# Sparse neighbour aggregation on one core: the adjacency matrix cut into units of 256 rows by all columns instead of 512 rows by half the columns

## The chip, the cores and the metric

The kernel runs on one core of one Trainium2 chip. The metric is device time in microseconds (us) of one execution, of which lower is better. A profiled execution gives a span (first to last instruction) that is a little shorter than that time.

## The reference

The inputs are node features `x` (4096 x 64), a dense adjacency matrix `adj` (4096 x 4096, fp32, only 0 and 1; 64 MB), a 64 x 64 weight and a bias. What is computed:

```python
h = relu(layernorm(x))
support = h @ weight                       # 4096 x 64
mask = (adj != 0)
rank = cumsum(mask, axis=1)
deg = rank[:, -1:]
k = minimum(deg, 100)
pos = rank - (deg - k)
w = mask * where(pos > 0, 0.5 ** (k - pos), 0.0)
out = x + (w @ support + bias)
```

So each neighbour is weighted by one half to the power of the number of neighbours to its right in the same row, and only the last 100 of a row count. The cumulative count along a row of 4096 columns is what couples the columns with each other.

## The kernel before

Nearly all of the data is `adj`. Row `r*2048 + p*16 + t` lies on partition p, so that one **tile** is 128 rows with the same `r` and `t` (32 tiles in all), and a partition's part of a tile is contiguous in memory.

The matrix is processed in 16 **units** of 512 rows (four tiles) by 2048 columns. For a group of 512 rows the right half of the columns comes first (the head), then the left half, since counts run from the right. For each unit:

- `load` (L120, SyncE queue): one 1 MB transfer for each tile, 8 KB on each partition, into one of 8 buffers (`a_sb`, pool `apool`). A load waits until the `convert` that read its buffer is done.
- `convert` (L341 on VectorE, L339 on ScalarE for three tiles): fp32 to one byte for each column, four columns to a word (`m8`, shown as `m`).
- `transpose` (L352, TensorE) turns 128 x 128 words through PSUM (`pt`), and `settle` (L363, VectorE) copies them to SBUF (`mt`): columns now lie on partitions, rows along the free axis.
- `totals` (L369) counts neighbours for each block of columns with matrix products; `split` (L379, ScalarE) and `divide` (L382, VectorE) each take one byte of the counts to fp16 (`sums`).
- `carry` (L388, GpSimd), in the left half alone, copies into a free row of `sums` what stands to the right of the unit, from the right half's `behind`.
- `suffix` (L396) adds up the later blocks with one matrix product for each byte, and `clamp` (L400, VectorE) makes the limited count `behind`.
- `place` (L407 and L412, TensorE), twice for a unit, forms the exponent codes in four PSUM banks (`v`, 5 buffers).
- `weigh` (L420, ScalarE), eight for a unit, takes two bytes of the code through Exp: 128 x 1024 weights (`wk`).
- `aggregate` (L453, TensorE), eight for a unit, multiplies the weights with `hr` (support as a high and a low fp32r part) into `acc`: two matrix products of 512 columns each.
- `drain`, `turn_back`, `finish` (L469, L476, L483 and L484) take each 512-row group out of PSUM, add x, and leave it for the stores.

Three of the last weighs (`QUICK`) are made on VectorE and GpSimd instead of ScalarE (`encode` L426, `take` L431, `lower` L439), and three others (`PARTED`) in halves of 256 rows. In front of all that stands a prologue (layer norm and support).

The order of the instructions on each engine is made in Python before the kernel is emitted: a planner holds for each step an engine, a duration and a due time, and always takes the step that can start soonest, among near ties the one due first. Each engine then works its list in order, so a step that waits holds up all behind it on its engine.

Of the kernel before, what the change touches and what calls it, by code (L numbers as in the profile page):

```python
# [29 lines left out]

@with_exitstack
def kernel(
# [12 lines left out]

# [7 lines left out]
    CB = HB // E  # L74
# [4 lines left out]
    G = RT // TG  # L79

    UNITS = [(g, c * P * E, n) for g in range(G) for c, n in ((4, 4), (0, 4))]
    U = len(UNITS)
    UT = [(u, tt) for u in range(U) for tt in range(TG)]
    NT = len(UT)
    POS = [sum(UNITS[v][2] for v, _ in UT[:n]) // 2 for n in range(NT + 1)]
    NP = 2 * CB
    QUICK = (U - 2, 4), (U - 1, 0), (U - 1, 4)
    PARTED = 5, 6, 7
    NA = 8
    NV = 5  # L90
    NB = 2
# [4 lines left out]
    bpool = ctx.enter_context(tc.tile_pool(name="bpool", bufs=6))  # L96
    mpool = ctx.enter_context(tc.tile_pool(name="mpool", bufs=3))
    wpool = ctx.enter_context(tc.tile_pool(name="wpool", bufs=NP + 4))
    dpool = ctx.enter_context(tc.tile_pool(name="dpool", bufs=2))
    bhpool = ctx.enter_context(tc.tile_pool(name="bhpool", bufs=3))  # L100
# [7 lines left out]


    tiles = {}  # L110
    xt = mpool.tile([P, CB, W, 2], F16, name="mt").rearrange("p c i e -> p (c i e)").bitcast(F32)
    xr = const.tile([P, H, HT, D], F32, name="xr")
    xr_v = x.rearrange("(r p t) d -> p r t d", r=H, t=HT)

    def load(n):
        u, tt = UT[n]
        g, c0, cb = UNITS[u]
        t = g * TG + tt
        tiles[n] = apool.tile([P, N // H], F32, tag="a_sb", name="a_sb")
        nc.sync.dma_start(tiles[n][:, :cb * E * P], adj_v[:, t // HT, t % HT, c0:c0 + cb * E * P])  # L120
# [9 lines left out]

# [13 lines left out]

    thr, later, excess = {}, {}, {}
    for cb in sorted({cb for g, c0, cb in UNITS}):
        thr[cb] = setup.tile([P, 4, SUB], F32, name=f"thr{cb}")
        later[cb] = const.tile([P, 2, P], F16, name=f"later{cb}")
        excess[cb] = const.tile([P, 1], F32, name=f"excess{cb}")
        nc.gpsimd.memset(thr[cb], 4096.0)  # L150
        nc.gpsimd.iota(thr[cb][:, :, 4:4 + 4 * cb].rearrange("p j (a f c) -> p j a f c", f=2, c=4),
                       pattern=[[1, 4]] + [[32, 2]] * (cb == CB) + [[16, 2], [4, 4]], base=0, channel_multiplier=0,
                       allow_small_or_imprecise_dtypes=True)
        nc.gpsimd.memset(thr[cb][:, :, 0:1], -1.0)
# [21 lines left out]

# [13 lines left out]
    over = setup.tile([P, 1], F16, name="over")  # L190
    nc.gpsimd.memset(over, 136.0)
    floor = const.tile([P, 1], F32, name="floor")
    nc.gpsimd.memset(floor, -38.0 * LN2)
# [4 lines left out]
    used = setup.tile([P, 2], F32, name="used")  # L198

    def order_of(cb):  # L200


        sub = setup.tile([P, 2], F32, name=f"sub{cb}")
        nc.vector.scalar_tensor_tensor(sub[:, 0:1], pf[:, 1:2], 8.0 if cb == CB else 2.0, pf[:, 3:4], op0=ALU.mult, op1=ALU.add)
        nc.vector.scalar_tensor_tensor(sub[:, 0:1], pf[:, 2:3], 0.125, sub[:, 0:1], op0=ALU.mult, op1=ALU.add)
        nc.vector.tensor_scalar(sub[:, 1:2], sub[:, 0:1], 16.0, None, op0=ALU.add)
        nc.vector.memset(sub[:1, 0:1], 4000.0)
        for f in range(2):
            nc.vector.tensor_scalar(later[cb][:, f, :], thr[cb].rearrange("p j r -> p (j r)"), sub[:, f:f + 1], used[:, f:f + 1],
                                    op0=ALU.is_lt, op1=ALU.mult)  # L210

    def constants(n):
        if n == 0:
            nc.vector.tensor_tensor(pi[:, 1:], pi[:, 0:1].to_broadcast([P, 5]), bits, op=ALU.bitwise_and)
            nc.vector.tensor_copy(pf, pi)
            nc.vector.tensor_scalar(used, pf[:, 5:6].to_broadcast([P, 2]), 8.0, None, op0=ALU.is_equal)
            nc.vector.memset(used[:1, 0:1], 1.0)

            nc.vector.tensor_scalar(one, row, 20.0, -1.0, op0=ALU.is_ge, op1=ALU.mult)
        elif n == 1:  # L220

# [15 lines left out]

# [8 lines left out]

# [3 lines left out]
    pxs, sqs, ns = {}, {}, {}  # L250

    def turn(h, t0):

# [9 lines left out]

        pxs[n] = ps_v.tile([P, W], F32, tag="v", name="pc")
        nc.tensor.matmul(pxs[n], less.rearrange("p h d -> p (h d)"), xt[:, n * W:(n + 1) * W], start=True, stop=True)  # L265

# [17 lines left out]

# [7 lines left out]

# [17 lines left out]
    def piece(h, i):  # L310
        return slice(h * HB + i * HB // 2, h * HB + (i + 1) * HB // 2)

    def first(h, i):
        nc.scalar.activation(hr[:, piece(h, i), 0, :], xs[:, piece(h, i), :], AF.Copy)

    def second(h, i):
        nc.vector.tensor_sub(hr[:, piece(h, i), 1, :], xs[:, piece(h, i), :], hr[:, piece(h, i), 0, :].bitcast(F32))

    def count(cb):
        r = SUB * cb  # L320
        px = pxs["count", cb] = ps_v.tile([P, W], F32, tag="v", name="pn")
        nc.tensor.matmul(px[:, :1], later[cb][:r, 1, :], over[:r], start=True, stop=True)
# [4 lines left out]

    low, codes, masks, words, wts, accs, tots, pts, sums8, behind, vs, signed = {}, {}, {}, {}, {}, {}, {}, {}, {}, {}, {}, (1, 7, 15)

    def convert(n):  # L330
        cb = UNITS[UT[n][0]][2]
        m8 = bpool.tile([P, CB * P, E], U8, name="m8")
        m_v, a_v = m8[:, :cb * P, :], tiles.pop(n)[:, :cb * P * E]
        if cb == CB:
# [3 lines left out]
        if n in signed:  # L338
# [3 lines left out]
        words[n] = m8  # L342

    def transpose(n, c0, c1):
        u, tt = UT[n]
        if tt == 0 and c0 == 0:
            masks[u] = mpool.tile([P, CB, W, 2], F16, name="mt")
        if c0 == 0:
            pts[n] = ps_t.tile([P, CB, P], F32, tag="t", name="pt")
        m32 = words[n].rearrange("p q e -> p (q e)").bitcast(F32)  # L350
        for c in range(c0, c1):
            nc.tensor.transpose(pts[n][:, c, :], m32[:, c * P:(c + 1) * P], ident)  # L352

    def settle(n):
        u, tt = UT[n]
        cb = UNITS[u][2]
        mw = masks[u].rearrange("p c i e -> p c (i e)").bitcast(U32)[:, :cb, tt * P:(tt + 1) * P]
        pt = pts.pop(n).bitcast(U32)[:, :cb, :]
        words.pop(n)
        if n in signed:  # L360
# [3 lines left out]

    def totals(u):
        tot = pts[u, "n"] = ps_t.tile([P, W], F32, tag="t", name="tot")
        for a in range(2):
            for c in range(UNITS[u][2]):
                nc.tensor.matmul(tot[SUB * c:SUB * (c + 1), :], band[:, SUB - 12 - 4 * a:2 * SUB - 12 - 4 * a],  # L369
                                 masks[u][:, c, :, a], start=(a == 0), stop=(a == 1), skip_group_check=True)  # L370

    def bytes_of(u, f):
        r = SUB * UNITS[u][2]
        if u not in sums8:
            sums8[u] = dpool.tile([P, 2, W], F16, name="sums8")
        return sums8[u][:r, f, :], pts[u, "n"][:r].bitcast(U8).rearrange("p (i f) -> p f i", f=4)[:, 1 + f, :]

    def split(u):
        nc.scalar.activation(*bytes_of(u, 0), AF.Copy)  # L379

    def divide(u):
        nc.vector.tensor_copy(*bytes_of(u, 1))  # L382

    def halved(u):
        pts.pop((u, "n"))

    def carry(u):
        nc.gpsimd.tensor_copy(sums8[u][:1, 0, :], behind[u - 1][:1, :])  # L388

    def suffix(u):  # L390
        cb = UNITS[u][2]
        r = SUB * cb
        sums = sums8.pop(u)
        px = pts[u, "s"] = ps_t.tile([P, W], F32, tag="t", name="ps")
        for f in range(2):
            nc.tensor.matmul(px, later[cb][:r, f, :], sums[:r, f, :], start=(f == 0), stop=(f == 1))  # L396

    def clamp(u):
        behind[u] = bhpool.tile([P, W], F16, name="behind")
# [295 lines left out]
```

## Time and profile before

The time is 190.65 us, median of 3 runs (190.29 to 190.69). The profiled execution has a span of 188.8 us.

| engine | busy us | share of the span | instructions |
|---|---|---|---|
| TensorE (PE) | 171.8 | 91% | 1499 |
| VectorE (DVE) | 161.7 | 86% | 221 |
| ScalarE (ACT) | 149.5 | 79% | 176 |
| GpSimd (POOL) | 20.4 | 11% | 60 |
| DMA | 69.49 MB moved | mean 368 GB/s | 10338 packets |

Busy time of TensorE counts the whole passage of each product, and products overlap, so TensorE is less full than its share says. A "mean ns" of a group is the time from start to end of one instruction; when the same engine goes on with the next, the distance from start to start is shorter. Both are given where they are used.

### The profile page before, as it was taken

The page shows a single profiled execution, that of the slowest core. Times are in us where ns is not written, and L with a number is a line of the kernel's source. Part 1 is how long each engine was busy: PE and PEld are TensorE (multiplying, and loading weights), DVE is VectorE, ACT ScalarE, POOL GpSimd, SP SyncE. Part 2 cuts the span into 40 slices and gives each one's busy share as a digit, 9 for nine tenths or more (in the row PEclk, how much of TensorE's full clock was granted, in tenths as well). Part 3 has the DMA queues.
Part 4 walks back from the last instruction along what each step waited for, and adds up shares of the span by engine and source line. Part 5 has one row for each costly group of instructions (what it writes and reads, how often), then busy time and mean ns, then how long its engine had stood idle before and what let it go on. Part 6 is the DMA issues. An engine that isn't in the chain of part 4 may idle for free.

```text
span 188.8 us, 3797 instructions
## 1 busy us (share of the span) xinstructions
PE 171.8 (91%) x1499; PEld 107.7 (57%) x1499; DVE 161.7 (86%) x221; ACT 149.5 (79%) x176; POOL 20.4 (11%) x60
## 2 busy tenths in 40 slices
PE   7879979898989999999979997999799999999980
PEld 5657746655555565466546554655366545554560
DVE  4834758899999999999999989998999899996743
ACT  2298055789899896999897889787978997899970
POOL 7000035020001000100020002000100029001000
PEclk9999687999999999999999999999999999999998
DMA  6999999999999999999999999999999999931000
GB/s 212 417 422 422 415 427 420 417 415 420 420 422 420 420 417 418 429 422 413 422 420 420 422 417 418 420 425 418 420 422 410 424 420 418 418 128 62 21 3 28
DMA packets 10338, 69.49 MB, mean 368 GB/s; under 512 B 1360, under 2 KB 1616, under 8 KB 2128
## 3 DMA queue, kind: packets, MB, share of 16 engines
q1 hardware_dynamic: 10016, 69.15, 88.6%
q8 instruction: 12, 0.20, 0.4%
q10 hardware_dynamic: 304, 0.10, 0.2%
q14 instruction: 6, 0.05, 0.1%
HBM read 68.19 MB, written 1.05 MB: 367 GB/s over the span
## 4 chain that ended last, share of the span: by engine, by line
PE 49%; DVE 29%; DMA 10%; ACT 5%; POOL 3%; issue 2%; POOLq 0%; ACTq 0%; DVEq 0%
PE acc L453 18%; DVE m L341 13%; DMA a_sb<-in_adj_dram 10%; PE pt L352 10%; DVE mt L363 6%; PE v L412 4%; PE v L407 4%; ACT wk L420 3%; PE pc L265 2%; PE tot L369 2%; PE pd L281 2%; PE ps L396 2%; DVE behind L400 2%; PE po L476 2%; ACT mt L260 1%
## 5 line engine op out<-in xcount | busy, mean ns | idle before, releaser
L420 ACT ACTIVATE wk<-v 128x1024 fp32r<-128x1024 uint8 (+1 forms) x128 | 120.0, 1015 | 15.3 <-PE v L412 14.9
L341 DVE TENSOR_SCALAR m<-a_sb 128x2048 uint8<-128x2048 f32 x61 | 84.9, 1394 | 4.2 <-DMA a_sb<-in_adj_dram 4.1
L453 PE MATMUL acc<-wk,hr 128*128 128x512 f32 (+1 forms) x256 | 77.7, 421 | 1.1 <-ACT acc_sb L469 0.6
L453 PEld LDWEIGHTS acc<-wk,hr 128*128 128x128 f32 x256 | 43.4, 189 | 18.6 <-issue 6.3
L352 PE MATMUL pt<-ident,m 128*128 128x128 f32 x256 | 41.2, 286 | 6.0 <-DVE m L341 5.4
L363 DVE COPY mt<-pt 128x512 uint32<-128x512 uint32 x61 | 41.7, 685 | 4.3 <-PE pt L352 4.3
L352 PEld LDWEIGHTS pt<-ident,m 128*128 128x128 f32 x256 | 29.7, 145 | 20.6 <-PE acc L453 4.8
L388 POOL COPY sums<-behind 1x512 f16<-1x512 f16 x8 | 6.8, 852 | 129.6 <-ACT sums L379 109.5
L407 PE MATMUL v<-behind,where 32*128 32x512 f16 x128 | 13.7, 383 | 1.5 <-DVE behind L400 1.1
L412 PE MATMUL v<-mt,tri 32*32 32x512 f16 x512 | 14.2, 394 | 0.0
L379 ACT ACTIVATE sums<-tot 128x512 f16<-128x512 uint8 x16 | 9.7, 608 | 3.5 <-PE tot L369 3.5
L400 DVE TENSOR_SCALAR behind<-ps,excess 128x512 f16<-128x512 f32 x16 | 11.9, 745 | 0.1
L382 DVE CAST sums<-tot 128x512 f16<-128x512 uint8 x16 | 10.9, 683 | 1.1 <-ACT sums L379 1.1
L369 PE MATMUL tot<-mt,band 128*32 128x512 f16 x128 | 10.2, 393 | 0.3 <-DVE mt L363 0.3
L396 PE MATMUL ps<-sums,later 128*128 128x512 f16 x32 | 10.0, 396 | 0.2 <-DVE sums L382 0.2
L407 PEld LDWEIGHTS <-where 32*128 32x128 f16 x128 | 3.7, 90 | 10.3 <-issue 9.8
L412 PEld LDWEIGHTS <-tri 32*32 32x32 f16 x512 | 4.4, 88 | 8.7 <-issue 8.7
L248 PE MATMUL none<-junk 128*128 128x256 bf16 x44 | 7.9, 362 | 1.1 <-DVE junk L133 1.1
L260 ACT ACTIVATE mt<-px 64x512 f32<-64x512 f32 x8 | 4.2, 585 | 4.9 <-PE px L256 4.8
L339 ACT ACTIVATE m<-a_sb 128x2048 int8<-128x2048 f32 x3 | 7.6, 2547 | 0.0
L248 PEld LDWEIGHTS <-junk 128*128 128x128 bf16 x44 | 5.6, 129 | 3.4 <-DVE junk L133 1.1
L272 ACT ACTIVATE xs<-pc 128x512 f32<-128x512 f32 x4 | 2.3, 610 | 6.0 <-PE pc L265 6.0
(87 smaller groups left out, 100.6 us busy)
## 6 DMA issues: line engine op xcount, KB each, us to landing
a_sb<-in_adj_dram SPq DMA_DIRECT2D x64, 1024.0 KB, 16.5
xr<-in_x_dram SPq DMA_DIRECT2D x2, 512.0 KB, 6.3
out_dram<-xr SPq DMA_DIRECT2D x1, 512.0 KB, 18.4
out_dram<-xr SPq DMA_DIRECT2D x1, 384.0 KB, 2.3
out_dram<-xr ACTq DMA_DIRECT2D x1, 64.0 KB, 1.6
out_dram<-xr SPq DMA_DIRECT2D x1, 64.0 KB, 1.7
w<-in_L_gnn_weight_dram ACTq DMA_DIRECT2D x2, 16.0 KB, 6.0
bias_sb<-in_L_gnn_bias_dram SPq DMA_DIRECT2D x1, 0.2 KB, 14.1
```

Of the source, the lines that this page charges most:

```text
L248: nc.tensor.matmul(none[:, :2 * P], junk[:, :P], junk, start=True, stop=True)
L341: nc.vector.tensor_scalar(m_v, a_v, 0.0, 64.0, op0=ALU.not_equal, op1=ALU.add)
L352: nc.tensor.transpose(pts[n][:, c, :], m32[:, c * P:(c + 1) * P], ident)
L363: nc.vector.tensor_copy(mw, pt)
L369: nc.tensor.matmul(tot[SUB * c:SUB * (c + 1), :], band[:, SUB - 12 - 4 * a:2 * SUB - 12 - 4 * a], masks[u][:, c, :, a], start=(a == 0), st ...
L382: nc.vector.tensor_copy(*bytes_of(u, 1))
L396: nc.tensor.matmul(px, later[cb][:r, f, :], sums[:r, f, :], start=(f == 0), stop=(f == 1))
L400: nc.vector.tensor_scalar(behind[u], pts.pop((u, "s")), excess[UNITS[u][2]], float(MAX_NEIGH), op0=ALU.subtract, op1=ALU.min)
L407: nc.tensor.matmul(v, where[q, a, :], behind[u][q, :], start=True, stop=False, skip_group_check=True)
L412: nc.tensor.matmul(vs[u, 4 * a + j][SUB * c:SUB * (c + 1), :], tri[q, q], m, start=False, stop=True, skip_group_check=True)
L420: nc.scalar.activation(wts[u, k][:, :, r], v.bitcast(U8).rearrange("p (i f) -> p f i", f=4)[:, :2, r], AF.Exp, scale=-LN2, bias=-38.0 * LN2)
L453: nc.tensor.matmul(accs[g][:, r], parts.rearrange("p s d -> p (s d)"), wk[:, s, r], start=(k == s == 0 and c0 + cb * E * P == N), stop=(c0 ...
```

## The change

A unit is now 256 rows (two tiles) by all 4096 columns. The right and the left half of a row stand side by side on the free axis as if they were different rows (virtual rows), so that a unit is still 512 wide and all matrix shapes up to `weigh` stay the same. It is for three things: a load can be a whole row (16 KB on each partition, 2 MB, 4 buffers), a conversion takes a whole row at once (128 x 4096), and what stands to the right of the left half is in the same unit, so that it is added by two more matrix products in `suffix` (`whole`: all blocks of the right half) and the carry through GpSimd falls away. Besides:

- `split` takes both bytes in one ScalarE instruction (128 x 1024); `divide` on VectorE is gone.
- `aggregate` needs different `hr` for the two halves: four products of 256 columns in place of two of 512.
- The last two tiles are made as three units: their right 2048 columns, then 1024, then 1024 columns, with loads of 1 MB, 0.5 MB and 0.5 MB for each tile. The last 512-row group is drained in three parts.
- `QUICK` and `PARTED` are gone: all weighs are on ScalarE. Two tile halves instead of three tiles are converted on ScalarE.
- x is fetched ahead of the first adjacency load; buffers: `m8` 4 of twice the size (was 6), `wk` 11 (was 12), `behind` 2 (was 3).
- The due times of all steps are new, and with them the order on each engine.

The core of the diff:

```diff
-    UNITS = [(g, c * P * E, n) for g in range(G) for c, n in ((4, 4), (0, 4))]
-    QUICK = (U - 2, 4), (U - 1, 0), (U - 1, 4)
-    PARTED = 5, 6, 7
-    NA = 8
+UNITS = [((t, t + 1), (16, 0), 4, ()) for t in range(0, 30, 2)]
+UNITS += [((30, 31), (16,), 4, ()), ((30, 31), (8,), 2, (15,)), ((30, 31), (0,), 2, (15, 16))]
+DRAINS = [(g, 0, 4, True) for g in range(7)] + [(7, 0, 2, True), (7, 2, 3, True), (7, 3, 4, False)]
+NA, NM, NW, NV, NB = 4, 4, 11, 5, 2
...
-        tiles[n] = apool.tile([P, N // H], F32, tag="a_sb", name="a_sb")
-        nc.sync.dma_start(tiles[n][:, :cb * E * P], adj_v[:, t // HT, t % HT, c0:c0 + cb * E * P])
+        if t not in tiles:
+            tiles[t] = apool.tile([P, N], F32, tag="a_sb", name="a_sb")
+        nc.sync.dma_start(tiles[t][:, c0 * P:c1 * P], adj_v[:, t // HT, t % HT, c0 * P:c1 * P])
...
-    def split(u):
-        nc.scalar.activation(*bytes_of(u, 0), AF.Copy)
-    def divide(u):
-        nc.vector.tensor_copy(*bytes_of(u, 1))
-    def carry(u):
-        nc.gpsimd.tensor_copy(sums8[u][:1, 0, :], behind[u - 1][:1, :])
+        nc.scalar.activation(sums8[u][:r, :, :w], pts.pop((u, "n"))[:r, :w].bitcast(U8).rearrange("p (i f) -> p f i", f=4)[:, 1:3, :],
+                             AF.Copy, bias=-68.0)
...
-        for f in range(2):
-            nc.tensor.matmul(px, later[cb][:r, f, :], sums[:r, f, :], start=(f == 0), stop=(f == 1))
+        todo = [(px[:, :w], later[cb][:r, f, :], sums8[u][:r, f, :w]) for f in range(2)]
+        for d in range(1, len(cols)):
+            todo += [(px[:, d * n:w], whole[cb][:r, :], sums8[u][:r, f, :w - d * n]) for f in range(2)]
+        for v in prior:
+            rv = SUB * UNITS[v][2]
+            todo += [(px[:, :w], whole[cb][:rv, :], sums8[v][:rv, f, :w]) for f in range(2)]
...
-        for s in range(2):
-            parts = low[u, k][:, s, :, :] if (u, k) in QUICK else hr[:, block(u, k) + 4 * s, :, :]
-            nc.tensor.matmul(accs[g][:, r], parts.rearrange("p s d -> p (s d)"), wk[:, s, r],
+        for s in range(2):
+            for a in range(ga):
+                for h, c0 in enumerate(cols):
+                    b = c0 + 8 * (a0 + a) + j + 4 * s
+                    o = a * w + h * n
+                    nc.tensor.matmul(accs[g][:, at:at + n], hr[:, b, :, :].rearrange("p s d -> p (s d)"), wk[:, s, o:o + n],
```

## The prediction

> **What bounds the kernel now.** I read the windows first: which engine or transfer is full in which stretch (columns: PE, PEld, DVE, ACT, POOL busy, granted clock, DMA share, GB/s).
>
> ```profile
> 45.00:65.00 20.00, 18.56 (x173) 11.24 (x172) 19.96 (x25) 18.75 (x21) 0.61 (x1) 1.00 1.01 421
> 125.00:145.00 20.00, 18.88 (x174) 11.34 (x172) 18.67 (x23) 17.19 (x21) 0.75 (x1) 1.00 1.01 417
> 160.00:168.00 8.00, 7.71 (x78) 4.40 (x76) 7.88 (x11) 7.31 (x9) 0.70 (x1) 1.00 0.83 344
> 168.00:178.00 10.00, 9.52 (x99) 5.60 (x84) 7.90 (x12) 9.20 (x12) 0.60 (x1) 1.00 0.12 44
> 178.00:189.00 11.00, 5.93 (x47) 3.86 (x45) 4.01 (x8) 5.05 (x9) 0.00 (x0) 0.94 0.05 13
> ```
>
> Until 167.4 us (end of the last 8 KB packet in the DMA records) the transfer is full: nothing makes the loads shorter except the loads. Behind them is a tail of 188.8 - 167.4 = 21.4 us. So the end is T, the last landing, plus a tail. VectorE is full at 45 to 65 us and eases later: it is behind the loads and catches up.
>
> Then the timeline, for what the tail consists of:
>
> ```profile
> 160.85 1.38 DVE L341 TENSOR_SCALAR m<-a_sb 128x2048 uint8<-128x2048 f32 x1
> ...
> 167.81 0.44 PE L412 MATMUL v<-mt,tri 32*32 32x512 f16 x16
> ...
> 168.40 1.94 ACT L420 ACTIVATE wk<-v 128x1024 fp32r<-128x1024 uint8 x2 [0.21 <-PE v L412]
> ...
> 172.57 3.78 ACT L420 ACTIVATE wk<-v 128x1024 fp32r<-128x1024 uint8 x4
> ...
> 176.67 5.97 ACT L420 ACTIVATE wk<-v 128x1024 fp32r<-128x1024 uint8 x9 [0.32 <-PE v L412]
> ...
> 182.14 0.63 PE L453 MATMUL acc<-wk,hr 128*128 128x256 f32 x4
> ```
>
> 168.40 is the first weigh of the last but one unit (u14), T + 1.0; from there ScalarE works nearly without a gap until 182.6, and 6.1 us of aggregate, drain and store follow. The last tile of u14 landed some 10 us before T, but was converted only at 160.85: 3 us late.
>
> The groups by form, for prices:
>
> ```profile
> L420 ACT ACTIVATE wk<-v 128x1024 fp32r<-128x1024 uint8 x122 | 116.9, 1035 | 15.2 <-PE v L412 14.9
> L341 DVE TENSOR_SCALAR m<-a_sb 128x2048 uint8<-128x2048 f32 x61 | 84.9, 1394 | 4.2 <-DMA a_sb<-in_adj_dram 4.1
> L363 DVE COPY mt<-pt 128x512 uint32<-128x512 uint32 x61 | 41.7, 685 | 4.3 <-PE pt L352 4.3
> L382 DVE CAST sums<-tot 128x512 f16<-128x512 uint8 x16 | 10.9, 683 | 1.1 <-ACT sums L379 1.1
> L388 POOL COPY sums<-behind 1x512 f16<-1x512 f16 x8 | 6.8, 852 | 129.6 <-ACT sums L379 109.5
> ```
>
> From start to start, engine kept busy, these are 0.906 (weigh; 0.479 for half of one), 1.276 (convert), 0.598 (settle), 0.597 us (divide); clamp 0.659, split 0.476, both adds of finish 0.79, drain 0.58. So a unit costs VectorE 4 x 1.276 + 4 x 0.598 + 0.597 + 0.659 + 0.79/2 = 9.15 us of the 10.0 in which its 4 MB arrive. First places of units 4 and 13 end at 74.8 and 159.2 us: 9.38 a unit. VectorE sets this pace, 0.6 us a unit faster than the loads.
>
> **What the Trainium skill says.** "DMA: Bandwidth & Descriptors", section "Where 436 GB/s comes from", gives a ceiling of 435.2 GB/s, and "Why small descriptors are slow" a fixed cost for each descriptor. The trace agrees: 421 GB/s in 8 KB packets at 312 ns, and 159 ns for the 4 KB packets of x, so twice 4 KB costs 6 ns more than 8 KB at once. "TensorE: Matmul & The Clock Gate", section "Step-by-step: what each phase is for", says that weight loads are pulled ahead of running products. The trace agrees: products of 256 columns, each with new weights, start 117 ns apart (four in 0.63 us above, with the passage of the last), those of 512 columns 232. "VectorE: DVE Perf Modes", "Specifications", gives 0.96 GHz; 2048 elements in 1.276 us are more than one a cycle, so I take two.
>
> **The change part by part.**
>
> 1. Loads. Before: 64 x 8 packets on each of 16 engines x 0.312 = 159.7, x 2.5, start 1.8: 164.0; the last engine ended at 167.4, so 3.4 of delays. After: 30 x 8 packets of 16 KB, 2 x 8 of 8 KB, 4 x 8 of 4 KB. A 16 KB packet is not in the trace: 2 x 312 - 6 = 618 ns by the step from 4 to 8 KB, or at least 602 ns by the skill's ceiling. With 618: 148.3 + 5.0 + 5.1 = 158.4, T = 166.1; with 602: T = 162.3. Delays kept. I take 615 and T = 165.4: 2 us less.
>
> 2. VectorE. A 4096-wide convert is 1.276 + 2048/(2 x 0.96) = 2.34 us (at most 2 x 1.276 = 2.55). A unit: 2 x 2.34 + 2.39 + 0.66 + 0.40 = 8.13. So 1.0 us less a unit, hidden behind the loads (9.9 us): worth only what VectorE was late at the end, 3 us before.
>
> 3. ScalarE. Split 0.476 becomes 0.906 (a weigh's size), so a unit is 8 x 0.906 + 0.906 + 0.29 = 8.44 (8.01 before), still under 9.9. Three QUICK weighs come back: 2.7 us, all of it in the tail.
>
> 4. TensorE. Aggregate 4 x 117 against 2 x 232: nothing. Suffix gains two products of 256 columns, 0.23 us a unit. Adding what its groups take in unhindered stretches, TensorE needed 8.4 us a unit, now 8.6: under 9.9, hidden.
>
> 5. Carry (0.85 us, beside the split and behind the clamp of the unit before) and divide's separate step go: they shorten the way from landing to weigh, not the pace.
>
> 6. Buffers: 4 loads of 4.9 us. A load waits for the convert four rows before, with nearly three loads queued, so VectorE may be about 12 us late before the DMA starves. It was up to 11 late at 35 us (tile landed 35.2, converted 46.7). x comes 2.5 us earlier, so I count nothing here; bound 0 to 3 us.
>
> 7. The tail, by the new order on each engine. Row 29 (end of u14) lands at T - 10.05 (4 MB behind it: 5.0 + 5.1); a convert began 0.6 us after the last packet where VectorE was waiting (13.3 us). From T - 9.45 VectorE has to do, before the clamp of u14: convert 2.34, finish 0.79, settle 0.60, convert 1.28 (row 30), two settles 1.20, convert 1.28 (row 31), settle 0.60, two converts of 1024 columns (0.53 + 0.21 = 0.74 each), settle 0.60, a third 0.74, then the clamp 0.66: 11.6 us, to T + 2.1. The early last tiles so stand in front of u14's clamp, and TensorE's place of u14 and all behind it waits too. Place to weigh is 0.9 us: first weigh of u14 at T + 3.0 (T + 1.0 before). From there ScalarE has 12 weighs x 0.906 + 8 half weighs x 0.479 + two splits of 0.48 + drains 0.58 and 0.35 = 16.6 us. The weighs are due one behind the other, PSUM refills while they run. After the last weigh: aggregate 0.5, drain 0.4, turning back 0.4, two pairs of adds 0.9, store 2.7 (186.13 to the end before): 4.9 against 6.1 before, since the last drain is smaller. Tail: 3.0 + 16.6 + 4.9 = 24.5 us.
>
> 8. The rest, at nothing: `whole` is two more 128x128 constants (0.34 us each, as `later`) while VectorE still waits for its first tile; two ScalarE converts for three save ScalarE 2.4 us in the prologue, where it waits; smaller `wk` and `behind` pools hold up TensorE only if ScalarE or VectorE is over eight steps ahead, and in the tail ScalarE is the last. PARTED only let the last weighs be aggregated in halves; the 256-row weighs of the last two units do the same.
>
> Sum: 165.4 + 24.5 = 189.9 us of span. Time is 1.85 above span (190.65 - 188.8): 191.75, say 191.7.
>
> **The rivals.**
>
> A, faster: the last units are smaller and VectorE is ahead, so the tail shrinks. For it: VectorE has 1 us spare a unit; the last load is 0.5 MB a tile. Against it: 16 weighs' worth stand behind u14's first in both kernels, now all on ScalarE, and it starts when row 29 is through. If packets go at 602 to 610 ns (T about 164) and the first weigh of u14 comes at T + 1.5, the span is 164 + 1.5 + 16.6 + 4.9 = 187.0: 188.8 us.
>
> B, no change: T falls by 2.5 to 3 us and the tail grows by as much. 164.6 + 24.2 = 188.8: 190.65 us.
>
> C, clearly slower: four large buffers and longer converts starve the DMA for 2 to 3 us in the prologue, or TensorE, 94% busy by its windows, can't take 0.23 us more a unit and u14 comes 2 us later still. 189.9 + 2.5 = 192.4: 194.3 us.
>
> **How the numbers follow.** Forecast (slightly slower, near 191.7): 0.37. A: 0.33. B: 0.13. C: 0.17. Faster 0.33, same 0.13, slower 0.37 + 0.17 = 0.54. The range must hold B and the forecast and most of A and C: 188.2 to 194.8. Its low end takes T = 163.5 with a tail of 22.9, its high end T = 166.1 with the forecast's tail and 2.3 us of stall.
>
> **What would show it.** Step 1: packets of 16 KB near 615 ns, last landing at 165.4. Step 2: convert 2.34 us from start to start, 128x4096. Step 4: acc 128x256 at 117 ns. Step 7: clamp of u14 behind the third 1024-column convert and its first weigh 3 us after the last landing, ScalarE gapless from there. I am wrong if that weigh begins before the last landing, if ScalarE has gaps in the tail or starts it far ahead, if T is at 163 or before, or if the DMA share falls below 1 in the middle.

## The result, and the profile after

The changed kernel takes 193.79 us (median of 4 runs, 193.17 to 194.25), the kernel before on the same chip 190.67 (190.29 to 190.80). The ratio is 1.0165, with a 95% interval of 1.0132 to 1.0198: about 3.1 us slower. The profiled span is 191.9 us against 188.8, so the profile shows the same 3.1 us.

First the windows of the changed kernel, in the stretches shown of before (busy PE, PEld, DVE, ACT, POOL, granted clock, DMA share, GB/s):

```profile
45.00:65.00 20.00, 18.99 (x207) 13.80 (x207) 18.25 (x18) 16.07 (x18) 0.00 (x0) 1.00 1.00 428
125.00:145.00 20.00, 19.17 (x209) 14.48 (x210) 17.88 (x17) 19.17 (x22) 0.00 (x0) 1.00 1.00 424
160.00:168.00 8.00, 7.52 (x96) 5.03 (x96) 8.00 (x12) 7.68 (x9) 0.00 (x0) 1.00 0.62 247
168.00:178.00 10.00, 10.00 (x146) 7.71 (x146) 3.90 (x9) 10.00 (x13) 0.00 (x0) 1.00 0.11 42
178.00:189.00 11.00, 9.90 (x104) 7.52 (x102) 2.31 (x8) 9.21 (x16) 0.00 (x0) 1.00 0.03 7
```

The loads did get faster: 424 to 428 GB/s where it was 417 to 421, and between 160 and 168 us there is less left to fetch. What got worse stands in the last two lines. Between 168 and 178 us TensorE was busy 9.52 us of 10 and ScalarE 9.20; now both are busy all the time. Between 178 and 189 us TensorE had 5.93 us to do and ScalarE 5.05; now it is 9.90 and 9.21. More work is left when the loads are over.

The timeline of the tail shows which work that is:

```profile
156.82 2.65 DVE L529 TENSOR_SCALAR m<-a_sb 128x4096 uint8<-128x4096 f32 x1
...
161.07 3.77 ACT L611 ACTIVATE wk<-v 128x1024 fp32r<-128x1024 uint8 x4 [0.32 <-PE v L605]
...
167.65 0.73 DVE L586 TENSOR_SCALAR behind<-ps,excess 128x512 f16<-128x512 f32 x1
...
168.80 3.88 ACT L611 ACTIVATE wk<-v 128x1024 fp32r<-128x1024 uint8 x4
...
185.11 2.06 ACT L611 ACTIVATE wk<-v 128x512 fp32r<-128x512 uint8 x4 [0.34 <-PE v L605]
```

156.82 is the convert of row 29, the last of unit 14; 167.65 that unit's clamp, which ends at 168.4. The row at 168.80 holds the last weigh of unit 13 and the first three of unit 14, whose first begins at 169.8. ScalarE ends its last weigh at 187.17. The last adjacency packet landed at 165.7 (T), so the tail is 26.2 us, where it was 21.4.

The chain that ended last, in order of time (start, duration, what), turns from loads to compute at one place and then never goes back:

```profile
130.06 16.30 DMA a_sb<-in_adj_dram
146.36 0.02 issue
146.38 2.66 DVE m L529
...
156.15 0.75 DVE behind L586
156.90 2.57 DVE m L529
...
165.22 0.66 PE pt L538 x4
...
178.13 1.05 ACT wk L611
```

The convert of row 27 at 146.38 is the last step that waits for a landing. From 165.22 to 178.08 the chain names TensorE alone; before and behind that it changes hands between VectorE, TensorE and ScalarE. (Where an engine has no gap, the chain follows it back instruction by instruction. ScalarE has no gap from 161.07 to 184.77 either, so the chain doesn't say which of the two sets the pace.)

The prices by form (times busy, mean ns of one; idle before, and its releaser):

```profile
L611 ACT ACTIVATE wk<-v 128x1024 fp32r<-128x1024 uint8 x124 | 118.4, 1048 | 16.9 <-PE v L605 16.7
L627 PE MATMUL acc<-wk,hr 128*128 128x256 f32 x512 | 81.0, 300 | 1.9 <-ACT wk L611 1.0 <-ACT acc_sb L639 0.5
L529 DVE TENSOR_SCALAR m<-a_sb 128x4096 uint8<-128x4096 f32 x26 | 68.8, 2645 | 0.3 <-DMA a_sb<-in_adj_dram 0.2
L567 ACT ACTIVATE sums<-tot 128x1024 f16<-128x1024 uint8 x15 | 15.6, 1042 | 1.9 <-PE tot L561 1.9
```

From start to start these are 0.905 (weigh), 0.118 to 0.120 (a product of 256 columns), 2.52 (convert) and 0.902 us (split).

Set side by side, the 3.1 us divide so: the first weigh of unit 14 comes 1.4 us later (169.8 for 168.4); from it to the end of the last weigh ScalarE takes 3.1 us more (17.4 for 14.25); the steps behind take 1.4 us less (4.7 for 6.1). 1.4 + 3.1 - 1.4 = 3.1. The granted clock is 1.00 in both tails up to 178 us, so it is no cause of this. The experiments ask why the first two grew although the loads ended 1.7 us earlier (165.7 for 167.4).

### The profile page after: what moved, and what is told of

It reads as the page before. It is cut to its first block, busy times and chain, and to the rows that moved or that the text cites. A ratio compares the mean times of both kernels' runs of the same rounds, so it can differ in the third digit from the quotient of the medians.

```text
span 191.9 us, 4285 instructions
## 1 busy us (share of the span) xinstructions
PE 176.6 (92%) x1815; PEld 130.0 (68%) x1815; DVE 150.7 (79%) x188; ACT 156.4 (82%) x182; POOL 8.8 (5%) x47
## 4 chain that ended last, share of the span: by engine, by line
PE 47%; DVE 20%; DMA 16%; ACT 12%; issue 3%; SPq 1%; ACTq 0%; DVEq 0%
PE acc L627 22%; DMA a_sb<-in_adj_dram 16%; DVE m L529 12%; ACT wk L611 10%; PE pt L538 8%; DVE mt L551 4%; PE tot L561 4%; PE v L605 4%; PE ps L581 3%; PE v L598 3%; PE pp L486 2%; DVE behind L586 2%; PE po L647 2%; ACT acc_sb L639 1%; ACT sums L567 1%
## 5 line engine op out<-in xcount | busy, mean ns | idle before, releaser
L611 ACT ACTIVATE wk<-v 128x1024 fp32r<-128x1024 uint8 (+1 forms) x132 | 122.5, 1021 | 17.2 <-PE v L605 17.1
L529 DVE TENSOR_SCALAR m<-a_sb 128x4096 uint8<-128x4096 f32 (+2 forms) x38 | 82.6, 2182 | 3.2 <-DMA a_sb<-in_adj_dram 3.1
L627 PE MATMUL acc<-wk,hr 128*128 128x256 f32 x512 | 81.0, 300 | 1.9 <-ACT wk L611 1.0
L627 PEld LDWEIGHTS acc<-wk,hr 128*128 128x128 f32 x512 | 67.3, 195 | 11.5 <-issue 5.7
L551 DVE COPY mt<-pt 128x512 uint32<-128x512 uint32 (+1 forms) x64 | 41.5, 669 | 10.3 <-PE pt L538 10.0
L586 DVE TENSOR_SCALAR behind<-ps,excess 128x512 f16<-128x512 f32 (+1 forms) x18 | 12.6, 702 | 11.1 <-PE ps L581 11.1
L567 ACT ACTIVATE sums<-tot 128x1024 f16<-128x1024 uint8 (+1 forms) x16 | 16.3, 1016 | 1.9 <-PE tot L561 1.9
L598 PE MATMUL v<-behind,where 32*128 32x512 f16 (+1 forms) x136 | 14.7, 371 | 1.1 <-ACT wk L611 1.1
L605 PE MATMUL v<-mt,tri 32*32 32x512 f16 (+1 forms) x544 | 14.5, 381 | 0.0
L561 PE MATMUL tot<-mt,band 128*32 128x512 f16 (+1 forms) x136 | 11.6, 407 | 0.9 <-DVE mt L551 0.8
L581 PE MATMUL ps<-sums,later 128*128 128x512 f16 (+1 forms) x32 | 9.4, 374 | 0.5 <-ACT sums L567 0.5
```

What stands on the lines that cost most here:

```text
L529: nc.vector.tensor_scalar(m_v, a_v, 0.0, 64.0, op0=ALU.not_equal, op1=ALU.add)
L551: nc.vector.tensor_copy(mw, pt)
L561: nc.tensor.matmul(tot[SUB * c:SUB * (c + 1), :w], band[:, SUB - 12 - 4 * a:2 * SUB - 12 - 4 * a], masks[u][:, c, :w, a], start=(a == 0), ...
L567: nc.scalar.activation(sums8[u][:r, :, :w], pts.pop((u, "n"))[:r, :w].bitcast(U8).rearrange("p (i f) -> p f i", f=4)[:, 1:3, :], AF.Copy, ...
L581: nc.tensor.matmul(o, l, m, start=(k == 0), stop=(k == len(todo) - 1), skip_group_check=True)
L586: nc.vector.tensor_scalar(behind[u][:, :w], pts.pop((u, "s"))[:, :w], excess[UNITS[u][2]], float(MAX_NEIGH), op0=ALU.subtract, op1=ALU.min)
```

## The experiments

Times are medians; each ratio is to the kernel before, on the same chip (190.7 to 190.9 us there). The changed kernel's own is 1.0165. The diffs are shortened to what matters.

### What the loads are worth

**8 KB packets again.** Each 2 MB load is cut in two of 1 MB, 8 KB on each partition; nothing else changes.

```diff
-        nc.sync.dma_start(tiles[t][:, c0 * P:c1 * P], ...)
+        for a, b in ((c0, mid), (mid, c1)):
+            nc.sync.dma_start(tiles[t][:, a * P:b * P], ...)
```

> The changed kernel with each 2 MB load issued as two of 8 KB on each partition. The packets go from 612 to twice 312 ns, so the last landing comes 240 x 12 ns = 2.9 us later at most. If the landing of the last rows sets the start of the tail: 1.5 to 3 us more, 195.3 to 196.8. If the compute engines are behind the loads all along (pace of 9.4 us a unit): within 0.7 us of 193.8, and the larger packets gain nothing.

Measured: 196.76 us, ratio 1.0298 (1.0268 to 1.0329), 3.0 us slower than with 16 KB (2.5 by the ratios). The rate between 45 and 65 us is 420 GB/s for 428. Units 6 to 9 begin to weigh 0.7 us earlier than in the changed kernel; unit 11 is 2.5 us later (145.2 for 142.7), unit 14 still 2.4 (172.2 for 169.8), and the last weigh ends at 189.6 for 187.2. Instructions of VectorE and TensorE on the way:

```profile
121.67 2.65 DVE L531 TENSOR_SCALAR m<-a_sb 128x4096 uint8<-128x4096 f32 x1 [1.57 <-DMA a_sb<-in_adj_dram]
...
132.94 2.64 DVE L531 TENSOR_SCALAR m<-a_sb 128x4096 uint8<-128x4096 f32 x1 [1.47 <-DMA a_sb<-in_adj_dram]
...
136.21 1.11 PE L540 MATMUL pt<-ident,m 128*128 128x128 f32 x4 [1.74 <-DVE mt L553]
...
139.07 0.42 DVE L656 TENSOR_TENSOR xr<-po,xr 128x256 f32<-128x256 f32 x1 [1.01 <-PE po L649]
```

Both converts wait about 1.5 us for a landing; the second, of row 24, is then 1.2 us later than in the changed kernel (131.71). The next one, of row 25, is 2.4 us later (139.87 for 137.42), although its row had landed 2.0 us before; from there on the distance stays at 2.2 to 2.4. In between TensorE stood 1.74 us, its granted clock was at half from 136.2 to 139.6, and VectorE waited for it. In the changed kernel the clock was 1.00 there. So the larger packets do save what they were made for, but a landing 1.2 us late accounts for about half of the delay in this execution; whether the slow stretch followed from the wait or came by chance was not tested. The changed kernel's loss comes from elsewhere and is larger.

**Products of 512 columns in the middle.** In units 1 to 14 the aggregates take 512 columns in one product, the left half of the columns multiplied with the right half's support (for timing only).

```diff
-                for h, c0 in enumerate(cols):
+                for h, c0 in enumerate(cols[:1]):
...
-                    nc.tensor.matmul(accs[g][:, at:at + n], ..., wk[:, s, o:o + n],
+                    nc.tensor.matmul(accs[g][:, 0:2 * n], ..., wk[:, s, o:o + 2 * n],
```

> The changed kernel with the aggregate of units 1 to 14 as two products of 512 columns with the right half's support for both halves, so that half as many products and weight loads are issued: the left half is weighed with the wrong support, a changed computation. Theory P (twice the products and weight loads fill TensorE): 2 to 3 us less, near 191. Theories S and D: within 0.7 us of 193.8.

Measured: 193.87 us, ratio 1.0153 (1.0127 to 1.0179), no difference to the changed kernel. The products gave no lead of their own, since two of 512 columns take as long as four of 256. But this execution happened to start earlier: its first weighs run ahead by 1.7 us at units 1 and 3, before the edit could add up to that, and the run with TensorE eased from unit 8 on (below) is 1.9 us ahead at unit 0, where its instructions are those of the changed kernel. So the lead is not the edit's. The granted clock points to where it came from: in the changed kernel it is at half from 35.9 to 42.8 us, here only from 35.8 to 39.2, and the lead of 1.7 us stands at unit 1, right behind that. What became of it is instructive: 1.8 us at unit 8 (112.1 for 113.9), 1.7 at unit 11, 0.2 at unit 12. One wait took it:

```profile
146.15 2.63 DVE L529 TENSOR_SCALAR m<-a_sb 128x4096 uint8<-128x4096 f32 x1 [1.57 <-DMA a_sb<-in_adj_dram]
```

This is row 27's convert again. What the compute had gained ahead of it was spent in waiting for that landing. A late start, by a slow clock or otherwise, is therefore no cause of the loss, and from here on only what lies behind row 27 matters: the last 20 us of loading and the tail.

### One engine at a time in the tail

**Three weighs back on VectorE and GpSimd.** The counterpart of QUICK: the last weigh of each half of unit 14 and the last of unit 15.

```diff
+QUICK = ((14, 0, 3), (14, 1, 3), (15, 0, 3))
...
+        if f == "weigh" and args in QUICK:
+            quick(*args)
+            continue
         does[f](*args)
```

> The changed kernel with three of the last weighs (one of four in each half of unit 14 and in unit 15) made on VectorE and GpSimd, as QUICK was before; the order of everything else is unchanged. Theory S (ScalarE's work after the first weigh of unit 14 sets the end): three weighs of 0.906 us leave ScalarE, so 2 to 2.7 us less than the changed kernel, about 191.3. Theory P (TensorE, full in the tail, sets the end): within 0.5 of 193.8. Theory D (the order on VectorE sets it): 193.8 or more, since VectorE gets 1.9 us a weigh.

Measured: 194.17 us, ratio 1.0165 (1.0144 to 1.0187): nothing gained. ScalarE, gapless before, now stops:

```profile
173.85 2.85 ACT L632 ACTIVATE wk<-v 128x1024 fp32r<-128x1024 uint8 x3 [0.52 <-PE v L626]
178.08 0.59 ACT L588 ACTIVATE sums_part<-tot 64x512 f16<-64x512 uint8 x1 [1.37 <-PE tot L582]
178.91 1.03 ACT L632 ACTIVATE wk<-v 128x1024 fp32r<-128x1024 uint8 x1 [0.24 <-PE v L626]
```

The 2.7 us taken off ScalarE come back as waits, and TensorE is named as the releaser of each. But the largest, 1.37 us, does not begin at TensorE. The moved weighs stand on VectorE, in front of the additions and of a settle:

```profile
173.49 1.22 DVE L518 TENSOR_SCALAR xs<-v 128x1024 int32<-128x1024 uint8 x1
...
176.58 0.41 DVE L572 COPY mt<-pt 128x256 uint32<-128x256 uint32 x1
...
176.81 0.41 PE L559 MATMUL pt<-ident,m 128*128 128x128 f32 x2 [0.87 <-DVE xr L680]
```

In the changed kernel the same settle begins 1.5 us earlier:

```profile
175.05 0.41 DVE L551 COPY mt<-pt 128x256 uint32<-128x256 uint32 x1
```

TensorE itself stood 0.87 us for VectorE, and the totals that ScalarE waited for came that much later. Only at the first wait, of 0.52 us, did TensorE have no gap. So theory P, a full TensorE, and theory D, the order on VectorE, both foresaw this time, and the run doesn't decide between them: it relieved ScalarE and loaded VectorE.

**The same in the kernel before, the other way round.** There QUICK is emptied, and the planner makes its order anew.

```diff
-    QUICK = (U - 2, 4), (U - 1, 0), (U - 1, 4)
+    QUICK = ()
```

> The kernel before with its three QUICK weighs made on ScalarE again and nothing else changed, planned anew. If giving up QUICK costs what ScalarE gets in the tail: 2 to 2.7 us more than before, 193 to 193.5, nearly the whole of the change's loss. If TensorE is as full there as in the changed kernel: within 0.7 us of before.

Measured: 192.46 us, ratio 1.0097 (1.0082 to 1.0112): 1.8 us slower. ScalarE is full nearly to the end, with fifteen weighs in one row:

```profile
172.48 12.00 ACT L420 ACTIVATE wk<-v 128x1024 fp32r<-128x1024 uint8 x15
184.58 0.47 ACT L469 ACTIVATE acc_sb<-acc,bias_sb 128x256 f32<-128x256 f32 x1
184.95 0.59 ACT L420 ACTIVATE wk<-v 128x512 fp32r<-128x512 uint8 x1
```

In the kernel before, moving three weighs away from ScalarE was worth 1.8 us. In the changed kernel the same move brought nothing in the order tried; an order planned for it was not run.

This run also shows what the changed kernel lost behind the first weigh of unit 14. With QUICK emptied, ScalarE takes 17.2 us from that weigh (168.32) to the end of the last (185.54), where with QUICK it took 14.2. That is the changed kernel's 17.4 but for 0.1 us, and both do 16 weighs' worth there. In the kernel before the return of the three weighs costs less in all than these 3.0 us, since the steps behind the last weigh take 5.2 us instead of 6.1.

**TensorE alone.** From unit 13 on, the second half of every weight tile is not aggregated: 5.7 us less on TensorE, all of it behind 161 us (half of each weight tile is left out of the sums).

```diff
-        for s in range(2):
+        for s in range(1 if u >= 13 else 2):
```

> The changed kernel in which units 13 to 17 leave out every second aggregate (the s = 1 blocks): 5.7 us of TensorE's products fall out of the tail, and that part of the sum is missing from the output. Theory C (TensorE and ScalarE are both full in the tail, so that relieving one alone gains nothing): 0 to 1 us less than 193.8. Theory P (TensorE alone sets the tail): 3 to 5 us less.

Measured: 194.58 us (193.39 to 195.54), ratio 1.02 (1.0151 to 1.0249); its interval overlaps the changed kernel's, and in its profile the last weigh ends at 186.8 for 187.2, 0.4 us earlier. In the window from 168 to 178 us TensorE falls to 8.47 us of 10 while ScalarE stays at 10.00. The four times differ by 2.1 us, and the two long ones had the lower mean clock (0.938 and 0.940, against 0.949 and 0.948); in the profiled execution the clock was at half from 182.2 to 185.6 us. So the time alone decides little here; the run from unit 8 on, below, has the clock at 1.00 through these stretches.

**Both.** The two edits above together.

> The same with three weighs moved from ScalarE to VectorE and GpSimd as in e1. Theory C: now both are relieved, so about 2 to 3 us less than 193.8, although e1 alone gained nothing. Theory P: no more than e5. Theory S (ScalarE alone) has fallen by e1.

Measured: 193.36 us (192.29 to 194.13), ratio 1.0135 (1.0093 to 1.0178); the profiled execution is 1.0 us shorter than the changed kernel's, the interval does not tell them apart. The 2 to 3 us that were expected did not come, and the removed work is 2.7 and 5.7 us. ScalarE still stops for code words from TensorE four times (0.37, 0.51, 0.30 and 0.23 us). As above, the moved weighs stand on VectorE in front of settles, so this run doesn't relieve the tail as a whole either.

### What sets the first weigh of unit 14

**VectorE's small converts out of the way.** Three of the converts of 1024 columns, which stand in front of unit 14's clamp, are put behind it.

```diff
+        if f == "convert" and args[0] in (36, 37, 38):
+            held.append(args)
+            continue
         does[f](*args)
+        if f == "clamp" and args == (14,):
+            for a in held:
+                convert(*a)
```

> The changed kernel with the three early 1024-column converts put behind the clamp of unit 14 on VectorE. Theory D (these converts hold up the clamp of unit 14, and with it the tail): the clamp ends about 2 us earlier, and 1 to 2 us are gained, 191.8 to 192.8. Theory S: ScalarE is busy with unit 13's last weigh until 169.7 in the profile of after, so the first weigh of unit 14 can move by at most about 1 us: 0 to 1 us gained. Theory P: nothing, 193.8.

Measured: 194.02 us, ratio 1.0159 (1.0135 to 1.0183), nothing gained. About 2 us of work are gone from in front of the clamp, and it ends only 0.2 us earlier:

```profile
166.27 0.69 DVE L551 COPY mt<-pt 128x512 uint32<-128x512 uint32 x1 [0.75 <-PE pt L538]
167.41 0.75 DVE L586 TENSOR_SCALAR behind<-ps,excess 128x512 f16<-128x512 f32 x1 [0.45 <-PE ps L581]
168.07 2.71 DVE L529 TENSOR_SCALAR m<-a_sb 128x1024 uint8<-128x1024 f32 x4
```

The clamp now waits for the suffix. There are two ways to it of nearly the same length: VectorE's list, and totals, split and suffix over TensorE and ScalarE. Nor could the clamp alone have moved the first weigh of unit 14: on ScalarE that follows the last weigh of unit 13 without a gap, here (170.2) as in the changed kernel (169.8).

**All converts half as wide.** Every convert of 4096 columns is made as two of 2048, and the planner makes its order anew with them.

```diff
-NARROW = 0, 1
+NARROW = range(U)
```

> The changed kernel with each 128x4096 convert made as two of 128x2048 at the same due times (8 buffers of half the size), planned anew. Theory G (converts of 2.5 us stand ahead of settles on VectorE and lengthen the way from landing to first weigh, 15 us at unit 13): 1 to 2.5 us less, 191.3 to 192.8. Rival: the length comes from TensorE's list, on which nothing changes: within 0.7 of 193.8.

Measured: 202.15 us, ratio 1.0608 (1.059 to 1.0626). This tells nothing of the width: the due times were made for other steps, the new order is bad all over (ScalarE waits 23.5 us in all for code words, 17.1 in the changed kernel), and the experiment is inconclusive.

**Half as wide, the order kept.** Only units 11 to 14, each second half behind the next short step of VectorE.

```diff
+        if h1 - h0 == 2 and u in HALVES:
+            for h in (1, 0):
+                late[n, 1 - h] = lambda h=h: nc.vector.tensor_scalar(m_v[:, h], a_v[:, h], ...)
+            late.pop((n, 0))()
...
+        if f != "convert" and late and f in ("settle", "clamp", "finish", "drain"):
+            for k in list(late):
+                late.pop(k)()
```

> The changed kernel, but the 4096-column converts of units 11 to 14 are made as two of 2048 columns, and the second stands behind the next settle (or other short step) of VectorE instead of in front of it. All else is in the same order, VectorE has the same work. Theory G (the 2.5 us converts in front of settles make the way from landing to first weigh longer): transposes and settles come up to 1.27 us earlier, first weigh of unit 14 at about 168.7 instead of 169.8, time 192.6 to 193.2. Theory T (TensorE's list): first weigh at 169.5 to 170.1, time 193.5 to 194.3, as changed.

Measured: 195.12 us, ratio 1.0236 (1.0222 to 1.0251), 1.3 us slower than the changed kernel; unit 14's first weigh comes at 171.6. Compare VectorE around one tile of that stretch, first in the changed kernel, then here:

```profile
127.38 2.65 DVE L529 TENSOR_SCALAR m<-a_sb 128x4096 uint8<-128x4096 f32 x1
130.32 0.69 DVE L551 COPY mt<-pt 128x512 uint32<-128x512 uint32 x1 [0.29 <-PE pt L538]
```

```profile
127.19 1.38 DVE L530 TENSOR_SCALAR m<-a_sb 128x2048 uint8<-128x2048 f32 x1
130.11 0.69 DVE L557 COPY mt<-pt 128x512 uint32<-128x512 uint32 x1 [1.54 <-PE pt L544]
130.72 1.39 DVE L530 TENSOR_SCALAR m<-a_sb 128x2048 uint8<-128x2048 f32 x1
```

The settle at 130 us waits for TensorE in both. The wide convert covered that wait; with half of it moved behind, 1.54 us stand empty. Theory G falls: the convert ahead of the settle is not what makes the way long. The rival's time, as changed, did not come either.

**TensorE eased from unit 8 on.** As the edit on TensorE above, but from unit 8, so that it also acts ahead of the last landing.

```diff
-        for s in range(2):
+        for s in range(1 if u >= 8 else 2):
```

> The changed kernel with the second half of every weight left out of aggregate for units 8 to 17 (each weight tile is multiplied once, not twice; for timing only). That is 8 x 4 x 0.118 / 2 = 1.9 us of TensorE less for each unit from unit 8 on, so TensorE is eased well before the last landing and not only behind it as in the earlier run (units 13 to 17). Theory T (TensorE's list holds up the way from landing to first weigh, 15.3 us at unit 13): the first weigh of unit 14 comes at 168.3 or before instead of 169.8, and the time falls to 192.3 or less. Theory G (VectorE's list with its 2.5 us converts in front of settles sets that way): first weigh of unit 14 at 169.5 to 170.1, time 193.5 to 194.3, as changed.

Measured: 193.08 us, ratio 1.0128 (1.011 to 1.0145). That is 0.7 us less than the changed kernel, with intervals that overlap, and lies between the two expectations. Unit 14's clamp ends at 168.0 (168.4) and its first weigh begins at 169.2 (169.8): half a microsecond, where TensorE had 1.9 us less to do in each unit. TensorE's list is not what sets this point. Behind it:

```profile
168.00:178.00 10.00, 8.50 (x123) 5.05 (x122) 3.51 (x8) 10.00 (x13) 0.00 (x0) 1.00 0.10 40
```

TensorE has room, the clock is at 1.00, and ScalarE is as full as before: from the first weigh of unit 14 to the end of the last 17.2 us pass for 17.4. So in the changed kernel it is ScalarE's own list that sets this stretch; easing TensorE, full beside it, shortened it by 0.2 us.

**ScalarE eased as well.** Besides, weigh makes only the half that is used.

```diff
+        ss = 1 if u >= 8 else 2
-        nc.scalar.activation(wts[u, a0, j][:, :, :w], ...[:, :2, :],
+        nc.scalar.activation(wts[u, a0, j][:, :ss, :w], ...[:, :ss, :],
```

> The run before last but one (second half of the weights not aggregated in units 8 to 17), and in those units weigh makes only the half that is used: 128 x 512 in about 0.48 us instead of 128 x 1024 in 0.906. So from unit 8 on TensorE has 1.9 us and ScalarE 3.4 us less for each unit, and neither can be the limit ahead of the last landing (for timing only: half the weights are left out). Theory V (from the landing of row 29 on, VectorE's list of 11.6 us in its fixed order, with the latency of the short steps between, sets the clamp of unit 14): clamp of unit 14 ends at 167.6 to 168.4 as changed, its first weigh starts near 169.0, and only the weighs behind it are shorter. Theory S (ScalarE, over 90% full in the units before, frees the code banks late, so place, transposes and the settles behind them come late): the first weigh of unit 13 comes 2 us or more ahead of 161.1 and the clamp of unit 14 ends at 166.5 or before. In either case the end falls by 0.43 us for each of some 15 weighs in the tail, up to 6 us, to 187 to 189; if TensorE's chain of the two last small units is the limit behind that, less.

Measured: 188.10 us, ratio 0.9883 (0.9855 to 0.9911), span 186.3. This run tells the two parts of the loss apart. First its window and its rows ahead of unit 14's weighs:

```profile
160.00:168.00 8.00, 6.45 (x68) 4.25 (x69) 8.00 (x12) 4.85 (x10) 0.00 (x0) 1.00 0.63 250
```

```profile
156.47 2.66 DVE L529 TENSOR_SCALAR m<-a_sb 128x4096 uint8<-128x4096 f32 x1
...
167.27 0.76 DVE L586 TENSOR_SCALAR behind<-ps,excess 128x512 f16<-128x512 f32 x1
...
169.00 1.58 ACT L612 ACTIVATE wk<-v 128x512 fp32r<-128x512 uint8 x3 [0.68 <-PE v L605]
```

ScalarE has 4.85 us to do in 8, TensorE 6.45, VectorE all 8.00. With both others eased that far, row 29's convert begins 0.35 us earlier than in the changed kernel, the clamp ends 0.4 us earlier, and the first weigh of unit 14 begins at 169.0 for 169.8. So VectorE's list, from the landing of row 29 on, sets the earliest time for this point (theory V): the second way, over totals, split and suffix, has become shorter, and the list remains. The other 0.8 us belong to the work that TensorE and ScalarE still have from unit 13. Behind it nearly all is different: the last weigh ends at 181.7, 12.7 us from the first, where it took 17.4. Those 4.7 us and the 0.8 are the gain. TensorE eased alone had brought 0.9 us of span (191.0), both together 5.6 (186.3). (The clock was at half from 125.1 to 131.9 us here, but row 27's convert begins at 146.48, right at its landing as in the changed kernel, so nothing of that is left.) ScalarE eased by as much with TensorE's work whole was not run; how far TensorE would then have held it up is open.

### A version that is faster than both

The end of the kernel before has two waits in it that the changed kernel doesn't have in this form:

```profile
183.33 0.50 PE L453 MATMUL acc<-wk,hr 128*128 128x256 f32 x2 [0.56 <-ACT acc_sb L469]
...
185.01 0.44 PE L476 MATMUL po<-ident,acc_part 128*128 128x128 f32 x2 [0.95 <-DVE xr L484]
```

The last aggregates wait until the first half is drained, and the second half is turned back only when the first has been read from the same PSUM tile. The edit on the kernel before gives each half a tile of its own, as the changed kernel does for its three parts, and puts the first drain behind the last aggregates:

```diff
-        if ("o", g) not in pts:
-            pts["o", g] = ps_t.tile([P, TG, 2, D], F32, tag="t", name="po")
+        if ("o", g, part) not in pts:
+            pts["o", g, part] = ps_t.tile([P, TG, 2, D], F32, tag="t", name="po")
...
+        if f is drain and args == (7, 0):
+            held.append(args)
+            continue
         f(*args)
+        if f is aggregate and args == (U - 1, 7, 1):
+            drain(*held.pop())
```

> The kernel before with two edits at its very end: the two halves of the last group are turned back into PSUM tiles of their own, and the drain of the first half stands behind the last aggregates in program order. In the kernel before, the last aggregates began at 183.33, when that drain had ended (0.76 us behind their weights), and the turning back of the second half began at 185.01, when the first half had been added (0.95 us of wait). If both waits go and nothing takes their place: 1.0 to 1.4 us less, 189.3 to 189.7. If only the second goes: 0.5 us less, 190.2. If the drain now waits for the last aggregates and the second drain for the first: no change, 190.7.

Measured: 190.14 us (189.97 to 190.52), ratio 0.9971 (0.9958 to 0.9983): 0.5 us faster than the kernel before. In the profiled execution the last weigh ended 0.7 us later than in that of before (183.30 for 182.64), so the spans are nearly the same (188.7 and 188.8); from there to the issue of the last store 2.8 us pass for 3.5:

```profile
183.89 0.47 ACT L469 ACTIVATE acc_sb<-acc,bias_sb 128x256 f32<-128x256 f32 x1 [0.60 <-PE acc L453]
184.40 0.48 DVE L467 TENSOR_SCALAR acc_part<-acc,bias_sb 128x256 f32<-128x256 f32 x1 [2.22 <-ACT acc_sb L469]
...
184.93 0.20 PEld L476 LDWEIGHTS po<-ident,acc_part 128*128 128x128 f32 x2 [0.32 <-DVE acc_part L467]
```

It is the middle case of the three expected. The turning back no longer waits for the additions, but the drain now waits for the last aggregates (0.60 us) and the second drain for the first, so the other wait has only moved.

## Why the prediction was right, and where its sums were off

The forecast was slightly slower, 191.7 us; 193.8 came, inside the range. The reason given holds: T falls, the tail grows by more. But the forecast loss was 1.0 us and the measured one 3.1: the sum of the tail was 1.7 us short. By its steps:

1. **Loads: right.** Packets of 16 KB took 612 ns (615 predicted), and the last landing came at 165.7 (165.4). With 8 KB packets it came 1.5 us later.
2. **VectorE: mis-sized, without effect.** The wide convert takes 2.52 us and not 2.34, nearly the upper bound of twice the narrow one: joining two saves almost nothing. The 2.34 came from the clock in the Trainium skill, "VectorE: DVE Perf Modes", section "Specifications", and two elements a cycle; the trace shows 1.63 elements a nanosecond, and the trace decides. In the tail's list errors cancel: from row 29's convert to the clamp 11.56 us were measured, 11.6 predicted, with 0.18 us more for the wide convert and 0.09 us less for each of three converts of 1024 columns (0.65 for 0.74).
3. **ScalarE: right in kind.** Split 0.902 (0.906 predicted), gapless from 161 to 184.8, then a gap of 0.34. Giving up QUICK is a cost: 1.8 us in the kernel before, as measured there. That it falls in the tail in full, 2.7 us of weighs, is right too: ScalarE's stretch there grew by 3.1 us, and with TensorE eased it stayed as long.
4. **TensorE: hidden, as far as the runs show.** The prices were right (0.118 for 0.117). With 1.9 us less for each unit from unit 8 on, unit 12 was 0.2 us ahead, the first weigh of unit 14 0.6, and the time 0.7 us less. But the step compared a unit's 8.6 us with the 9.9 of its loads and did not look at the tail, where no loads come: between 168 and 178 us TensorE has no gap at all. There it is nearly as full as ScalarE, and would have held up a lighter ScalarE by an amount that no run shows.
5. **Carry and divide: the shorter way is not seen.** From the last landing of unit 13 to its first weigh 15.3 us passed, about 12 before. The order and the sizes of other steps on this way changed too, so what the two steps were worth by themselves is not shown.
6. **Buffers: nearly right at nothing.** The DMA share is 1.00 in the windows from 45 to 145 us. In the prologue it fell to 0.92 once, from 35 to 40 us (385 GB/s); from the rates between 30 and 45 us (416 GB/s on average, for 428 later) an estimate is 0.4 us of loading lost, about the 0.3 by which the last landing is late.
7. **The tail: right in its order, short by 1.7 us.** The first weigh of unit 14 came at T + 4.1, not T + 3.0. Of these 1.1 us 0.6 are the clamp's (T + 2.7 for 2.1): row 29's convert began that much later than assumed, behind unit 13's clamp. The other 0.5 lie between clamp and weigh (1.45 us for 0.9): ScalarE still had the last weigh of unit 13 to do, until 169.9. Where TensorE and ScalarE were eased, unit 14's first weigh came 0.8 us earlier. From there to the end of the last weigh 17.4 us passed for 16.6, of which one gap is 0.34; the end took 4.7 for 4.9. So the span is off by 0.3 (T) + 1.1 + 0.8 - 0.2 = 2.0 us: 191.9 for 189.9.
8. **The rest: right at nothing.** The time is again 1.9 us above the span.

Rival A failed at T (165.7, not about 164) and at the first weigh, which came at T + 4.1 and not at T + 1.5. Rival B had the fall of T too large (2.5 to 3 us for 1.7) and the growth of the tail too small (4.8 us were measured). Rival C's time was the nearest, 194.3, but by chance: of its reasons, the DMA was starved for about 0.4 us and not for 2 to 3, unit 14 came 1.1 us later than forecast and not 2, and easing TensorE took 0.6 of that back.

So the 3.1 us come from two places. The stretch of weighs grew by 3.1 us, and counting ScalarE's instructions there at their start-to-start prices gives the parts: 2.77 us more of weighs (12 whole and 8 halves for 10 and 6), 0.97 for a split and a drain more, and 0.63 less of waiting and the rest. The first weigh of unit 14 came 1.4 us later, of which VectorE's list accounts for 0.6 and the work of TensorE and ScalarE from unit 13 for 0.8, as the run with TensorE and ScalarE eased shows. The shorter end gave 1.4 us back.

What stays open: why unit 13 takes 15.3 us from its last landing to its first weigh, where before it took about 12. TensorE eased by itself shortens it by 0.3 us, TensorE and ScalarE together by 1.6, and the split converts made it longer. It may be the fixed alternation of the engines that remains, but no run made a better order of the same steps, so this is argued and not shown. Nor was an order tried in which three weighs leave ScalarE of the changed kernel without standing in front of VectorE's settles.

## What to carry to other kernels

When loads bound a kernel, a faster load moves the last landing by what it saves, and the tail behind it decides what of that remains: count, for each engine, the work still left at the last landing, not its share over a unit. When a run moves work off a full engine and gains nothing, follow each new wait back past the engine it names: the work may have landed in front of something that the first engine needs. Taking work out of one engine without giving it to another, as was done for TensorE here, is the cleaner test of whether it sets the pace. A step that stands ahead of a wait may be covering it, so try a new order before believing that the long step is the delay.

## What the hardware showed beyond that

The conversion from fp32 to one byte on VectorE has hardly any fixed part: 0.65, 1.27 and 2.52 us from start to start for 1024, 2048 and 4096 columns. Packets took 159, 313 and 612 ns for 4, 8 and 16 KB, so doubling 8 KB saves 14 ns, more than the 5 ns that doubling 4 KB does, and 2% of the rate. An fp32r product of 256 columns with new weights costs half of one of 512 (0.117 to 0.120 against 0.230 to 0.240 us), so cutting products in two was free for TensorE.

The granted clock was at half in stretches of 3.4, 6.8 or 10.2 us, mostly in the first 43 us, and not at the same times in every execution: in the profiled one of the changed kernel from 18.9 to 25.7 and from 35.9 to 42.8 us. In the second of these a product of 256 columns took 0.213 us from start to start instead of 0.120. Unit 1 then begins up to 1.7 us later, and of this little is left at the end where a wait for a landing lies between.
